# Near attention of a metaformer: the exponential, the spreading and the write at other steps of the pipeline

## The chip, the cores and the metric

The kernel runs on one core of a Trainium2 chip. The metric is the device time of one execution in microseconds (us). A core has five engines with an instruction queue each: PE (matmul), DVE (VectorE), ACT (ScalarE), POOL (GpSimd) and SP (SyncE), which in this kernel issues transfers. Sixteen DMA engines carry the transfers.

## The reference

Four layers of a metaformer work on an image batch `x` of shape (4, 64, 64, 128). The change touches the first half of layer 0 alone, a deformable attention in which each pixel attends to nine sampled pixels, in four groups of 32 channels with dilations 1, 3, 5 and 7. Cut to what matters:

```python
qkv = conv2d_depthwise(x @ w_qkv + b_qkv)
mask = sigmoid(conv1x1(pconv(q_img, pconv_mask_w), w_mask, b_mask))
for i in range(4):
    off = conv1x1(pconv(q_img, pconv_off_w[i]), w_off[i], b_off[i])
    dil = 2 * i + 1
    k_list.append(deform_sample(kv[0, :, i], off, mask, dil, dil * PAD))
    v_list.append(deform_sample(kv[1, :, i], off, mask, dil, dil * PAD))
...
attn = softmax(einsum('bgnc,bgckn->bgnk', qf, ks_), axis=-1)
out = einsum('bgnk,bgckn->bgnc', attn, vs_)
return out @ w_proj + b_proj
```

`deform_sample` samples bilinearly at a tap's place plus its learned offset and multiplies by the mask. The other layers (an expert-choice FFN, a triangle update and a recurrent layer, a Fourier attention and a pair attention, each with a mixture of experts) are the same in both kernels.

## The kernel before

When no offset is larger than 1, the kernel takes `deformable_near`. There every tap reads a 3 x 3 neighbourhood of its undisplaced place, so a query's keys and values lie in a fixed window, and bilinear sampling is a weighting with "hat" functions of the offset.

The work is cut into 128 steps; one step is two image rows, 128 query pixels, which lie on the 128 partitions. Four steps make a chunk `c`; there are 32 chunks, eight for each of four images. One loop over `T` runs all stages of the pipeline at once. What a pass does for step `T` or for a chunk is told by `step(T, first, do, every)`: it calls `do(n)` for `n = (T - first) / every` where that is a whole number in range. In order of a chunk's life:

- Four passes of `product` (L773, PE): products of queries and keys in PSUM `S`; `copy_products` (L783, ACT) moves them to `band`, of which there are two sets. `products` (L744, ACT) prepares the next queries.
- `hats_of_rows` and `hats_of_columns` (ACT, L700, L704), `masked` and `hat_products` (POOL, L722, L731) make the interpolation weights `H`, two buffers.
- At step 4c+4, `attention` (L785 to L812, DVE): shift the bands by predicated copies (L792), weight with `H` and reduce to logits `lg` (L794, L801), subtract the largest (L809 to L811).
- At step 4c+7, `spread` (L814 to L836): the exponential on ACT (L817), then on DVE the sum, the reciprocal and the scaling (L818 to L820), then `A`, the weight of each pixel of the window: nine products (L824) for dilations 3, 5 and 7, three into `shared` (L830) and a reduce (L834) for dilation 1. `A` has two buffers.
- At step 4c+9, `write` (L841, SP): four transfers of `A` to a ring of three buffers `dd` in DRAM.
- At `LAG - 2` = 12 steps after its own number, `read_dense` (L850, SP): four transfers bring a step's rows back from `dd` as a dense matrix `D`, four buffers in turn. This turns a layout by query into one by key.
- At `LAG` = 14 steps after its own number, `values`, `transpose` (L884 on PE, L886 on ACT) and `weigh` (L904, PE) multiply `D` with the values `vb` (L862, SP, seven buffers); after every fourth step, `values_done` (L916), `projection` (L925 to L929) and `store` (L936, SP) finish a chunk. The residual `xg` is loaded by SP (L876) into two buffers in turn; its buffer is free once the store of the chunk before last has landed.

SP also loads queries (`q`, L759), offsets (`of`, L696) and keys (`kpad`, L752). All of SP's transfers stand in one queue, in the order in which they are built.

Within one pass the order of the engines' instructions is set by two means: the order of the calls, and `tc.issue_after`, which keeps what is built inside it from going ahead of a named instruction. `behind()` names the last block of PE; `after[0]` is the last copy of products of this pass. Otherwise a scheduler orders instructions by what they wait for, so an instruction need not stand where its call does.

Of the kernel before, what the change touches and what calls it, by code (L numbers as in the profile page):

```python
# [12 lines left out]
AF = mybir.ActivationFunctionType  # L13
# [347 lines left out]
def window(ap, off, dims):  # L361

    return bass.AP(ap.tensor, ap.offset + off, [list(ap.ap[0])] + dims)


def stage_deformable(k, x, y, w_qkv, b_qkv, w_dw, b_dw, pconv, w_offT, b_off, grid, masks, w_proj, b_proj):

    nc, tc = k.nc, k.tc
    with ExitStack() as octx:  # L380
        dr = octx.enter_context(tc.tile_pool(name="da_d", bufs=1, space=DRAM))
        fp = octx.enter_context(tc.tile_pool(name="da_f", bufs=1))
        qd = [dr.tile([128, 4096], F32, tag=f"qd{b}", name=f"qd{b}") for b in range(4)]
        kd = [dr.tile([128, 4096], F32, tag=f"kd{b}", name=f"kd{b}") for b in range(4)]
        vd = [dr.tile([80, 84, 128], F32, tag=f"vd{b}", name=f"vd{b}") for b in range(4)]
        od = [dr.tile([128, 32, 81], F32, tag=f"od{b}", name=f"od{b}") for b in range(4)]
        far = deformable_project(k, fp, x, qd, kd, vd, od, w_qkv, b_qkv, w_dw, b_dw, pconv, w_offT, b_off)
        with tc.If(far > 0) as branch:
            deformable_general(k, x, y, w_qkv, b_qkv, w_dw, b_dw, pconv, w_offT, b_off, grid, w_proj, b_proj)
        with branch.Else():  # L390
            deformable_near(k, dr, x, y, qd, kd, vd, od, masks, w_proj, b_proj)
# [217 lines left out]
def deformable_near(k, dr, x, y, qd, kd, vd, od, masks, w_proj, b_proj):  # L609
# [19 lines left out]
    nc, tc = k.nc, k.tc  # L629
# [5 lines left out]
    with ExitStack() as ctx:  # L635
# [44 lines left out]
        Hs, bands, outs, vblocks, logits, ofs, hat_of, queries = {}, {}, {}, {}, {}, {}, {}, {}  # L680
# [3 lines left out]
        def behind():  # L684

            return tc.issue_after(last[0].ins) if last[0] is not None else ExitStack()

        def block(do, *args):

            with behind():  # L690
                last[0] = do(*args)
# [32 lines left out]
        def hat_products(c, groups):  # L724

            if 0 in groups:
                Hs[c] = sm.tile([128, 4, 36, 12], F32, tag="H", name="H")
            H = Hs[c]
            hy, hx, _ = hat_of[c]
            for g in groups:  # L730
                nc.gpsimd.tensor_tensor(  # L731
                    H[:, g].rearrange("p n (a c) -> p n a c", a=4), window(hy, 144 * g, [[4, 36], [1, 4], [0, 3]]),
                    window(hx, 108 * g, [[3, 36], [0, 4], [1, 3]]), op=ALU.mult,
                )

        def products(T):
            i = T % 32
            c, t = divmod(T, 4)
            if t == 0:
                bands[c] = [sm.tile([128, 3, 4, 4, CW[g]], F32, tag=f"band{g}", name=f"band{g}") for g in range(4)]  # L740
            qm = qms[T % 2]
            q = queries[T // 4]
            for h in range(2):
                nc.scalar.copy(  # L744
                    window(qm, 256 * h, [[32, 2], [72, 4], [1, 8]]),
                    q[:, 2 * (i % 4) : 2 * (i % 4) + 2, 32 * h : 32 * h + 32].rearrange("p y (m x) -> p y m x", m=4),
                )

        def rows_of_keys(n):

            b, h = divmod(n, 4)
            nc.sync.dma_start(  # L752
                kpad[:, 8 + 16 * h : 24 + 16 * h, 8:72], kd[b].rearrange("p (y x) -> p y x", x=64)[:, 16 * h : 16 * h + 16, :]
            )

        def rows_of_queries(n):
            b, h = divmod(n, 8)
            queries[n] = sm.tile([128, 8, 64], F32, tag="q", name="q")
            nc.sync.dma_start(queries[n], qd[b].rearrange("p (y x) -> p y x", x=64)[:, 8 * h : 8 * h + 8, :])  # L759
# [25 lines left out]
        def attention(c):  # L785
# [25 lines left out]
            nc.vector.tensor_tensor(lg, lg, each, op=ALU.subtract)  # L811
            logits[c] = lg, m, me, taps, wide, each  # L812

        def spread(c):  # L814
            H = Hs.pop(c)
            lg, m, me, taps, wide, each = logits.pop(c)
            nc.scalar.activation(lg, lg, AF.Exp, scale=32 ** (-0.5))  # L817
            nc.vector.tensor_reduce(m, taps, axis=AX.XY, op=ALU.add)  # L818
            nc.vector.reciprocal(me, wide)
            nc.vector.tensor_tensor(lg, lg, each, op=ALU.mult)  # L820
            A = As[c % 2]
            for g in range(1, 4):
                for ty in range(3):
                    nc.vector.tensor_tensor(  # L824
                        window(A[g], ty, [[12 * DIL[g], 12], [3, 4], [12, 3]]), window(H, 432 * g + 144 * ty, [[12, 12], [3, 4], [1, 3]]),
                        window(lg, 36 * g + 12 * ty, [[1, 12], [0, 4], [0, 3]]), op=ALU.mult,
                    )

            for tx in range(3):
                nc.vector.tensor_tensor(  # L830
                    window(shared, 13 * tx, [[60, 12], [3, 4], [12, 3]]), window(H, 12 * tx, [[36, 12], [3, 4], [1, 3]]),
                    window(lg, tx, [[3, 12], [0, 4], [0, 3]]), op=ALU.mult,
                )
            nc.vector.tensor_reduce(  # L834
                window(A[0], 0, [[1, 3], [60, 4], [3, 20]]), window(shared, 0, [[240, 3], [60, 4], [3, 20], [1, 3]]), axis=AX.X, op=ALU.add
            )  # L836
# [96 lines left out]
        def store(some):  # L933
            for o in some:
                _, b, c, xg = o
                nc.sync.dma_start(tokens(y, b, 4 * c, 4), xg)  # L936
                stores.remove(o)

        def step(T, first, do, every=1):
            n = T - first  # L940
            if 0 <= n < 128 and n % every == 0:
                do(n // every)

        LAG = 14
        for h in range(4):
            rows_of_keys(h)
        rows_of_queries(0)
# [2 lines left out]
        products(0)  # L950
        for T in range(128 + LAG):
            now[0] = T
            with behind():
                step(T, -1, products)
                step(T, -5, offsets, 4)
                step(T, 2, masked, 4)
                step(T, 2, lambda c: hat_products(c, (0, 1)), 4)
                step(T, 3, lambda c: hat_products(c, (2, 3)), 4)
                step(T, 4, attention, 4)
                step(T, 7, spread, 4)  # L960
                step(T, 9, write, 4)
                step(T, LAG - 2, read_dense)
                step(T, LAG, values)
            V, P = 0 <= T - LAG, T < 128
            late = [o for o in stores if o[0] <= T - 2]
            if V:
                block(transpose, T - LAG)
            if P:
                block(product, T)
            if project:  # L970
                block(projection, *project.pop())
            if V:
                block(weigh, T - LAG)
            with behind():
                store(late)
                step(T, 0, copy_products)
                with tc.issue_after(after[0].ins):
                    step(T, 0, hats_of_rows, 4)
                    step(T, 1, hats_of_columns, 4)
                step(T, LAG, values_done)  # L980
                if T % 4 == 1 and T < 124:
                    rows_of_queries(T // 4 + 1)
                if T < 96:
                    b, i = divmod(T, 32)
                    for h in range(4):
                        if i == min(8 * h + 13, 31):
                            rows_of_keys(4 * (b + 1) + h)
# [1639 lines left out]
```

## Time and profile before

| what | us |
|---|---|
| three runs: lowest, median, highest | 7522.86, 7536.76, 7555.75 |
| profiled execution: its time | 7520.84 |
| profiled execution: its span | 7519.0 |
| near stage in the span | about 680 to 1668 |
| of it: first writes of A to the ring (L841) | 731.20, 753.21, 775.93, 796.84 |
| of it: 26 chunks, from the write at 829.27 to that at 1583.50 | 754.23 |
| busy in those 754.23: PE, DVE, ACT, POOL | 627.95, 594.68, 423.87, 191.34 |
| busy share of the whole span: PE, DVE, ACT, POOL | 86%, 64%, 38%, 20% |

Three views are used below. The page is one profiled execution in numbers: busy time, 40 slices of the span, the costliest groups. A view of waits says for one engine what its idle time ended on, added up. A timeline lists runs of equal instructions in order of start: start, duration, engine, line, operation, output, inputs, and in square brackets the idle time before it with what ended it. For SP the duration is the time in which its queue hands the transfers out. `L841` is line 841 of the kernel before. The near stage is an eighth of the time, so shares over the whole span say little about it; windows inside it do.

### The profile page before, as it was taken

Reading aid. Unit: us, or ns where it says so; the run is one execution under the profiler, and the core shown is the slowest. Engines: PE = TensorE matmul, PEld = TensorE weight load, DVE = VectorE, ACT = ScalarE, POOL = GpSimd, SP = SyncE. Lnnn points to the kernel's source line nnn. Section 1 sums busy time; section 2 is a strip of 40 time slices with the busy share of each in tenths; the row PEclk is TensorE's granted clock in tenths of the full one; section 3 lists DMA queues with packets and bytes.
Section 4 is the critical chain, followed back from the end, with each engine's and each line's share of the span. In section 5 each row is a group of like instructions: output and inputs, shape, how many; then the busy total and the mean of one; then the engine's idle time right before and its main releaser. Section 6 shows DMA issues by size and latency. Waiting matters only on the chain. (4 is left out here: it accounts for less than half of the span.)

```text
span 7519.0 us, 156903 instructions
## 1 busy us (share of the span) xinstructions
PE 6475.0 (86%) x63791; PEld 3490.8 (46%) x63791; DVE 4812.9 (64%) x10774; ACT 2842.8 (38%) x6717; POOL 1518.8 (20%) x1218
## 2 busy tenths in 40 slices
PE   7996888866688789799989988798897997998989
PEld 3443666654455553255555555445224234252244
DVE  2113877754577437588756566674885876857877
ACT  3332555543243326411156665564013022040055
POOL 0001222210011100055522221253012111120135
PEclk9997888987889899899989899797997997988989
DMA  4436788871300130300000000001111111111101
GB/s 120 98 89 195 210 246 242 244 227 60 137 1 2 34 67 9 116 23 23 25 10 9 9 10 4 9 1 42 34 25 50 26 39 34 27 32 41 23 23 31
DMA packets 673783, 498.10 MB, mean 66 GB/s; under 512 B 296822, under 2 KB 588600, under 8 KB 669208
## 3 DMA queue, kind: packets, MB, share of 16 engines
q1 hardware_dynamic: 510158, 399.80, 18.9%
q10 hardware_dynamic: 162890, 88.11, 4.4%
q8 instruction: 509, 8.34, 0.5%
q14 instruction: 226, 1.85, 0.1%
HBM read 335.28 MB, written 152.33 MB: 65 GB/s over the span
## 5 line engine op out<-in xcount | busy, mean ns | idle before, releaser
L2496 DVE TENSOR_TENSOR t<-S,q 128x1536 f32<-128x1536 f32 (+3 forms) x608 | 1157.0, 1949 | 120.7 <-PE S L2484 115.5
L2484 PE MATMUL S<-R,L 32*128 32x512 f32 x4096 | 734.6, 651 | 90.1 <-DMA R<-wd 78.6
L2512 PE MATMUL acc<-t,sum 128*32 128x512 f32 x4096 | 639.6, 608 | 0.0
L2198 PE MATMUL pe<-ew,yT 128*128 128x512 f32 x1024 | 480.6, 604 | 25.2 <-DVE xs L2204 22.3
L1797 PE MATMUL acc<-w,attT 128*64 128x264 f32 x4096 | 485.2, 390 | 11.0 <-DVE w L1793 11.0
L2484 PEld LDWEIGHTS S<-R,L 32*128 32x128 f32 x4096 | 200.4, 186 | 611.2 <-issue 280.1
L2518 ACT COPY agg<-acc 128x512 f32<-128x512 f32 x32 | 18.8, 586 | 1192.6 <-DMA L<-pd 855.4
L792 DVE COPY_PREDICATED band<-bit,band 128x384 f32<-128x384 int32 (+11 forms) x384 | 312.5, 929 | 186.4 <-ACT band L783 149.8
L773 PE MATMUL S<-kpad,qm 32*64 32x192 f32 (+3 forms) x8192 | 365.8, 405 | 72.4 <-ACT band L783 37.7
L2204 DVE SCALAR_TENSOR_TENSOR xs<-pe,gate,xs 128x128 f32<-128x128 f32 x1024 | 333.1, 346 | 96.9 <-PE pe L2198 80.3
L1790 POOL TENSOR_TENSOR w<-xtl,ei 128x528 f32<-128x528 f32 x256 | 332.1, 1319 | 310.5 <-ACT ei L1789 202.5
L1793 DVE TENSOR_TENSOR w<-xtl,pe 128x1056 f32<-128x1056 f32 x256 | 320.4, 1251 | 99.5 <-ACT ei L1789 88.6
L1797 PEld LDWEIGHTS acc<-w,attT 128*64 128x64 f32 x4096 | 283.5, 137 | 197.1 <-DVE w L1794 38.3
L2207 ACT ACTIVATE sc<-pe,gate 128x128 f32<-128x128 f32 x1024 | 291.2, 375 | 199.5 <-PE pe L2198 192.4
L773 PEld LDWEIGHTS S<-kpad,qm 32*64 32x64 f32 x8192 | 265.6, 151 | 128.8 <-issue 65.3
L514 PE MATMUL dw<-pad,diag 32*32 32x512 f32 x6912 | 307.4, 612 | 13.2 <-issue 7.3
L884 PE MATMUL pt<-ident,D 128*128 128x128 f32 x1536 | 259.8, 319 | 66.3 <-DMA D<-dd 48.4
L2512 PEld LDWEIGHTS acc<-t,sum 128*32 128x32 f32 x4096 | 92.7, 108 | 458.4 <-issue 436.1
L2198 PEld LDWEIGHTS pe<-ew,yT 128*128 128x128 f32 x1024 | 185.6, 193 | 232.1 <-issue 151.5
L2527 POOL TENSOR_TENSOR o<-o,bf 128x512 f32<-128x512 f32 x32 | 40.7, 1271 | 1228.5 <-ACT o L2526 1228.5
L886 ACT COPY dt<-pt 128x512 f32<-128x512 f32 x384 | 205.5, 595 | 146.2 <-PE pt L884 145.7
L884 PEld LDWEIGHTS pt<-ident,D 128*128 128x128 f32 x1536 | 214.6, 203 | 87.6 <-DMA D<-dd 52.3
(520 smaller groups left out, 12716.7 us busy)
## 6 DMA issues: line engine op xcount, KB each, us to landing
vb<-vd SPq DMA_DIRECT2D x272, 256.0 KB
D<-dd SPq DMA_DIRECT2D x128, 192.0 KB
D<-dd SPq DMA_DIRECT2D x128, 168.0 KB
D<-dd SPq DMA_DIRECT2D x128, 144.0 KB
w<-in_e_weight_dram ACTq DMA_DIRECT2D x16, 1024.0 KB
w<-in_e_weight_dram SPq DMA_DIRECT2D x16, 1024.0 KB
wd<-s SPq DMA_DIRECT2D x32, 512.0 KB
D<-dd SPq DMA_DIRECT2D x128, 120.0 KB
```

What stands on the lines that cost most here:

```text
L514: nc.tensor.matmul(acc[g][32 * c : 32 * c + 32], diag[r, j, tap, :], pads[j][r, y0 : y0 + 8, tx : tx + 64], start=(tap == 0), stop=(tap == 8),
L773: ins = nc.tensor.matmul(acc[g][64 * h : 64 * h + 64].rearrange("p (a s) c -> p a s c", a=3), qm[rows, h, m, :], keys, start=(m == 0), sto ...
L792: nc.vector.copy_predicated(flat[:, :, 0:n], bit[:, 0, :, i : i + 1].to_broadcast([128, 48, n]), flat[:, :, s : s + n])
L884: ins = nc.tensor.transpose(pt[:, g, :], D[:, g, ty : ty + 382 : 3], k.ident)
L1790: nc.gpsimd.tensor_tensor(w2[:, 2:4], xt[:, 2:4, 0:2], window(ei, 0, [[0, 2], [0, 2], [1, 132]]), op=ALU.mult)
L1793: nc.vector.tensor_tensor(w1, xt[:, :, 1:3], window(pe, 0, [[0, 4], [0, 2], [1, 132]]), op=ALU.mult)
L1797: nc.tensor.matmul(acc[b // 2][64 * (b % 2) : 64 * (b % 2) + 64], attT[:, b // 2, hp, 64 * (b % 2) : 64 * (b % 2) + 64], src[:, b].rearran ...
L2198: nc.tensor.matmul(pe[h].rearrange("p e c -> p (e c)"), yT[:, 128 * t : 128 * t + 128], ew[:, 4 * h : 4 * h + 4, :].rearrange("p e c -> p ...
L2204: nc.vector.scalar_tensor_tensor(xt, pe[0][:, e, :], gate[:, t, e : e + 1], xt, op0=ALU.mult, op1=ALU.add)
L2484: nc.tensor.matmul(S[:, j, :], Ls[n % 2][r, ag, :], Rs[n % 2][r, ag].rearrange("p x y -> p (x y)"), start=True, stop=True)
L2496: nc.vector.tensor_tensor(t[:, j0:j1].rearrange("p u (x y) -> p u x y", x=8), S[:, j0:j1].rearrange("p u (x y) -> p u x y", x=8), qf[:, q0 ...
L2512: nc.tensor.matmul(acc[0][32 * h : 32 * h + 32, :], sum4, t[:, j, :], start=(u < 4), stop=(u >= 60))
```

## The change

`spread` is split. The exponential becomes a function of its own, `exponential`, and is issued at step 4c+7 inside the `issue_after(after[0])` at the end of the pass, that is, not ahead of that pass's last copy of products. The rest of `spread` is issued one step later (4c+8), `write` one step later (4c+10). `LAG` is 15, so that the values of a step are used one step later, and the loop has 143 passes in place of 142. `read_dense` stays at twelve steps after its own number, now `LAG - 3`: a step's dense rows are read three steps ahead of their use. The number of buffers, the instructions and the transfers are the same. Of the built order on DVE it can be said that the logits of chunk c+1 now stand between those of chunk c and the spreading of chunk c.

```diff
--- before.py
+++ after.py
@@ -811,10 +811,13 @@
             nc.vector.tensor_tensor(lg, lg, each, op=ALU.subtract)
             logits[c] = lg, m, me, taps, wide, each
 
+        def exponential(c):
+            lg = logits[c][0]
+            nc.scalar.activation(lg, lg, AF.Exp, scale=32 ** (-0.5))
+
         def spread(c):
             H = Hs.pop(c)
             lg, m, me, taps, wide, each = logits.pop(c)
-            nc.scalar.activation(lg, lg, AF.Exp, scale=32 ** (-0.5))
             nc.vector.tensor_reduce(m, taps, axis=AX.XY, op=ALU.add)
             nc.vector.reciprocal(me, wide)
             nc.vector.tensor_tensor(lg, lg, each, op=ALU.mult)
@@ -941,7 +944,7 @@
             if 0 <= n < 128 and n % every == 0:
                 do(n // every)
 
-        LAG = 14
+        LAG = 15
         for h in range(4):
             rows_of_keys(h)
         rows_of_queries(0)
@@ -957,9 +960,9 @@
                 step(T, 2, lambda c: hat_products(c, (0, 1)), 4)
                 step(T, 3, lambda c: hat_products(c, (2, 3)), 4)
                 step(T, 4, attention, 4)
-                step(T, 7, spread, 4)
-                step(T, 9, write, 4)
-                step(T, LAG - 2, read_dense)
+                step(T, 8, spread, 4)
+                step(T, 10, write, 4)
+                step(T, LAG - 3, read_dense)
                 step(T, LAG, values)
             V, P = 0 <= T - LAG, T < 128
             late = [o for o in stores if o[0] <= T - 2]
@@ -977,6 +980,7 @@
                 with tc.issue_after(after[0].ins):
                     step(T, 0, hats_of_rows, 4)
                     step(T, 1, hats_of_columns, 4)
+                    step(T, 7, exponential, 4)
                 step(T, LAG, values_done)
                 if T % 4 == 1 and T < 124:
                     rows_of_queries(T // 4 + 1)
```

## The prediction

> **What bounds the kernel now.** The change touches one stage, the near attention of layer 0, so I read the page's 40 slices first. This is their DMA row:
>
> ```profile
> DMA  4436788871300130300000000001111111111101
> ```
>
> A slice is 188 us. Slices 4 to 8 (about 680 to 1668 us of the span) are the near stage, and nowhere else is DMA so busy. The view of windows gives an undisturbed piece of it (columns: us, busy PE, PE weight load, DVE, ACT, POOL, TensorE clock, DMA share, GB/s):
>
> ```profile
> 1100.00:1350.00 250.00, 203.89 (x5847) 167.06 (x5847) 193.65 (x381) 140.89 (x421) 59.67 (x58) 0.89 0.81 242
> ```
>
> PE at 82%, DVE at 77% and DMA at 81%: three near-ties, no compute engine full. So I read who waits, between 830 and 1580 us, in the views of waits of ACT, PE and SP (waited for: us, times, longest):
>
> ```profile
> ACT lg L817 <- DVE lg L811: 84.4, 23, 6.3
> ```
>
> ```profile
> PE out L904 <- issue: 40.2, 31, 3.3
> PE pt L884 <- DMA D<-dd: 38.6, 54, 3.1
> ...
> PE S L773 <- ACT band L783: 5.2, 6, 2.1
> ```
>
> ```profile
> SPq L876 <- DMA x<-xg: 49.1, 23, 2.8
> ```
>
> The first line is what catches the eye: ACT stands 84.4 us for the logits before the exponential, with the copies of PE's products behind it. But PE, which would have to suffer from that, waits for ACT only 15.5 us in that stretch (5.2 here; 6.9, 2.6 and 0.8 in lines of that view not shown). It waits longer for dense rows. One such place, in the timelines of ACT, PE and DVE:
>
> ```profile
> 1196.01 0.32 ACT L817 ACTIVATE lg<-lg 128x144 f32<-128x144 f32 x1 [4.94 <-DVE lg L811]
> ```
>
> ```profile
> 1195.36 0.35 PE L884 MATMUL pt<-ident,D 128*128 128x128 f32 x1 [3.05 <-DMA D<-dd]
> ```
>
> ```profile
> 1200.63 3.11 DVE L830 TENSOR_TENSOR shared<-H,lg 128x144 f32<-128x144 f32 x3
> 1203.77 0.90 DVE L834 TENSOR_REDUCE A<-shared 128x240 f32<-128x720 f32 x1
> ```
>
> ACT's 4.94 us end at 1196.0, but PE stood for D until 1195.4. Two stalls lie side by side, and removing ACT's moves nothing there. Why D is late shows in SP's queue, one chunk of it:
>
> ```profile
> 1180.12 4.16 SPq L841 DMA_DIRECT2D dd<-A  x4
> 1184.38 2.00 SPq L862 DMA_DIRECT2D vb<-vd  x2
> 1186.47 0.54 SPq L696 DMA_DIRECT2D of<-od  x1
> 1187.06 1.26 SPq L862 DMA_DIRECT2D vb<-vd  x2
> 1188.52 3.46 SPq L850 DMA_DIRECT2D D<-dd  x4
> 1192.06 0.41 SPq L759 DMA_DIRECT2D q<-qd  x1
> 1192.58 1.41 SPq L936 DMA_DIRECT2D x<-xg  x1
> 1194.08 2.60 SPq L850 DMA_DIRECT2D D<-dd  x4
> 1199.33 0.39 SPq L876 DMA_DIRECT2D xg<-in_x_dram  x1
> 1199.82 3.10 SPq L862 DMA_DIRECT2D vb<-vd  x4
> 1203.01 5.30 SPq L850 DMA_DIRECT2D D<-dd  x8
> 1208.41 4.95 SPq L841 DMA_DIRECT2D dd<-A  x4
> ```
>
> From write to write is 28.29 us. The rows hold dd 4.16, vb 2.00 + 1.26 + 3.10, D 3.46 + 2.60 + 5.30, small loads 0.54 + 0.41 + 1.41 + 0.39: 24.63 in all. 2.65 is a hole (1196.68 to 1199.33: the xg load waits for an x store), 1.0 small gaps. DVE had A ready at 1204.67 (1203.77 + 0.90), and SP came for it at 1208.41, 3.7 us later. In this stretch I find SP 1 to 16 us behind DVE at every write. The transposes of D(57) ended at 1178.2, and the next rows for that buffer were issued at 1194.1, 16 us after it came free. So SP's queue, an in-order list of transfers that keeps the DMA engines at 0.81, sets the end of a chunk; DVE, ACT and, mostly, PE are pulled along. From the write at 829.27 to the one at 1583.50 are 26 chunks: 29.0 us each.
>
> **What the Trainium skill says.** "DMA: Bandwidth & Descriptors", section "Anatomy of one DMA — SWDGE (gpsimd) path": a semaphore wait happens on the issuing sequencer before dispatch, the DMA engines only consume their queues. It is stated for another path; the hole of 2.65 us before the xg load, with vb and D behind it, shows the same on SP. "SBUF — State Buffer", section "Who interferes with whom": a VectorE operation with two SBUF inputs contends with GpSimd reads, a tensor_reduce never. The trace agrees: three shared products took 3.11 us above, beside POOL, and 0.94 at 1610.59 us, alone; the reduce took 0.90 both times.
>
> **The change, part by part.** No instruction is added or removed: 32 exponentials, 128 writes and 512 dense reads in either kernel. All of it is order.
>
> 1. The exponential of chunk c goes from step 4c+7 ahead of the copies, where the built order puts it before the copy of step 4c+5, to behind the copies of step 4c+7. ACT's wait of 84.4 us goes. What is late next: PE's rows of D, at the same time. Of the 15.5 us that PE waits for ACT I count 5.2 + 0.8 as owed to the exponential and give a third of it, 2 us, to the end; the rest is bought by D.
>
> 2. Spread moves behind the following attention. DVE's work per chunk was 15.16 (attention, 1180.81 to 1195.97) + 0.40 (exponential) + 8.30 (spread, to 1204.67) = 23.9 us. The 0.40 goes. In the built order the tail of attention c+1 and the head of spread c are interleaved, and POOL's products of H for chunk c+2 must wait for the buffer that spread c reads, so the overlap on shared (3.11 against 0.94) and on the nine A products (3.26 against 2.45) mostly goes: up to 3.0 us of DVE. DVE isn't the bound: 0. If that cover is gone (SP faster), it would be worth up to 3.4.
>
> 3. Write one step later, in chunk time: A is ready about 21 us after attention c+1 starts, 24 if the contention stays. Read by steps, from A's end to the write is about as much as before, 0 to 3 us more. The write stands in SP's queue with the 16 reads of the next chunk and the vb loads behind it; if it has to wait, they all do. Seen slack 1 to 16 us, so 0, bounded by 0 and 2 us a chunk.
>
> 4. LAG 15 with reads at T - 12: the same step in the loop, so the reads are not moved in it, but each is used one step later, and the write, one step later too, still comes five steps ahead of the first use. The four D buffers come free one step later relative to the read. SP is 16 us behind that already, so 0. One drain step more: the drain at the end (1610 to 1650 us) is itself paced by D reads, 5.3 us per two steps, and one write now stands right before the reads that need it: about +3 us once.
>
> 5. SP's order, from the built kernels: before, write, 2 vb, of, 2 vb, D4, q, x, D4, xg, 4 vb, D8; after, write, 2 vb, q, of, D4, 2 vb, D4, 2 vb, x, D4, xg, 2 vb, D4. The same 16 D, 8 vb, 4 writes, the same bytes; vb is spread out, and the xg load still follows one D4 after the store. The hole of 2.65 stays, 0; bounded by -1 (more time between store and load) and +2.2 (below).
>
> 6. Start: up to 797 us SP does wait for A: its writes begin at 731.20, 753.21, 775.93 and 796.84, so DVE sets the pace at about 22 us. After, the first A is finished some 16 us later, but the copies of chunk 1 no longer stand behind the first exponential (5.37 us) and the second (4.79), and values start a step later. By my count of steps the first transpose comes at about 762 instead of 766.8: -5 us, once, bounded by -7 and +10.
>
> Sum: -2 - 5 + 3 = -4 us. Against the profiled execution's 7520.84 (span 7519.0 + 1.84): 7517. The median of the runs shown is 7536.76, 15.9 above that execution; against it the same -4 gives 7533.
>
> **The rivals.** *Faster: the ACT stall is the bound after all.* For it: 84.4 us over 23 chunks is 3.7 each, PE is the busiest engine, and its 40.2 us of "issue" ahead of L904 have no visible cause. If a chunk is set by PE, it can fall from 29.0 towards its busy time, 24.2 (627.95 over the 26 chunks, by the view of windows), plus 2.5 of issue gaps (65.3 over 26): 26.7. Against it: the DMA share, and SP behind DVE at each write. I take 2 us a chunk over 28 chunks: -56, 7481.
>
> *Slower: SP's new order makes the x round trip dearer.* A pair of vb and, in about 12 chunks, a kpad load now stand ahead of the store. If SP's in-order wait for the store (2.65 us) grows by the time that two more vb need (2 x 256 KB at 242 GB/s is 2.2 us), and kpad, whose following four vb took 5.74 us at 1109.5 against 3.10 here, falls on it, a chunk costs 2.2 more: 28 x 2.2 = +62, 7599. It decides from 1.35 us a chunk (38 over 28). Against it: what is ahead of the store isn't between the store and the load.
>
> *Slower: the write waits for DVE.* Slack of 3.7 us here, at times 1. If the spread moved behind an attention takes SP from 3.7 ahead to 1.3 short in each chunk, 27 x 1.3 = +35: about 7570.
>
> **How the numbers follow.** 0.5% of 7536.76 is 38 us, about what a measurement of this kernel can tell from no change: same is 7499 to 7574. The forecast, 7533, has 0.63; the faster rival 0.20; the two slower ones 0.12 and 0.05. The forecast's own range, from the bounds of parts 3, 5 and 6, is 7505 to 7565, mostly same. The second slower rival straddles the border and gives 0.01 to same; so faster 0.20, same 0.64, slower 0.16. The range over all, 7487 to 7587, leaves out half of the faster rival and most of the first slower one.
>
> **What would show it.** Right: the chunk from dd write to dd write stays at 28.5 to 29.5 us; ACT's wait at L817 falls below 10 us; PE's waits for D and its issue gaps stay or grow by as much as its waits for ACT shrink; shared takes about 1 us; SP still arrives after A is done. The first rival: a chunk of 27 us or less with PE above 85%. The second: the wait of L876 above 100 us in the stage. The third: SP's dd write waiting for DVE L834 in most chunks. The forecast is wrong if the near stage, 988 us, changes by more than 38.

## The result, and the profile after

The changed kernel takes 7559.47 us (median of 7 runs, 7545.16 to 7572.25); the kernel before, in its runs beside it, 7536.76 (7 runs). The ratio is 1.0032, with a 95% interval of 1.0016 to 1.0048: slower by about 23 us, where 4 us less was forecast. The profiled execution of the changed kernel took 7557.5 us (span 7555.5) against 7520.84.

Where the time went can be read from the first transposes of single steps (line 884 before, 887 after). The first of step 0 starts at 759.9 us (before 766.8), that of step 8 at 814.3 (823.0), of step 116 at 1619.8 (1599.5), of step 127 at 1687.7 (1658.8). So the start is 8.7 us earlier, the 27 chunks in between lose 29 us, about 1.1 each, and the drain loses another 8.6. Up to the first transpose of step 127 this is +28.9 of the 36.7 by which the two profiled executions differ; the rest comes after it. From here on "a chunk" is the mean from step 24 to step 112, 22 chunks: 29.15 us before, 30.09 after. These are means of one profiled execution each. Two of the experiments below, `xg3` and `late_vshape`, left SP's order as it is before and after, and had 29.22 and 30.11, so differences below about 0.1 us say nothing.

The same window as before, in the changed kernel (columns as there):

```profile
1100.00:1350.00 250.00, 198.01 (x5566) 159.56 (x5566) 176.42 (x361) 134.04 (x399) 63.40 (x57) 0.86 0.83 233
```

PE and DVE are less busy than before (203.89 and 193.65), and the DMA share has risen from 0.81 to 0.83, while the rate fell from 242 to 233 GB/s. DMA is busier for fewer bytes. The granted TensorE clock between steps 24 and 112 was lower, 0.876 in place of 0.895. That is not what cost the time: `xg3` had 0.876 too, with the chunk of before.

The views of waits, 830 to 1580 us, of PE, ACT and SP:

```profile
PE pt L887 <- DMA D<-dd: 80.1, 101, 3.1
PE out L907 <- issue: 35.6, 21, 3.9
PE out L907 <- DMA vb<-vd: 14.5, 3, 5.9
```

```profile
ACT qm L744 <- PE S L773: 168.8, 96, 3.5
ACT dt L889 <- PE pt L887: 161.5, 114, 5.9
```

```profile
SPq L939 <- POOL H L731: 40.2, 12, 6.1
SPq L879 <- DMA x<-xg: 35.1, 17, 3.1
```

ACT's wait for the logits, 84.4 us before, is not in its list any more; ACT now waits for PE alone. PE's waits for ACT's copies of 15.5 us are gone too, but its wait for dense rows has doubled, from 38.6 to 80.1.

SP's first line is new: the store of x (L939) is held in SP's queue, for POOL by this view. POOL is unlikely to be what it waits for: the store handed out for 5.63 us from 1229.30 on had its result from POOL at 1213.75. The ten long ones among these stores all stand right behind a load of keys (`kpad`, L752), and what stands there was handed out slowly before as well (2.5 to 3.8 us, now 4.6 to 6.3). Nor is it where the time was lost: from write to write, the ten chunks with a load of keys (of chunks 4 to 28) took 31.1 us before and 31.4 after, the fifteen without one 27.8 and 29.3. With other transfers of SP's queue as marks, the chunks without one still lose 1.0 to 1.4 us.

DVE does what was expected of it (timeline):

```profile
1200.71 0.92 DVE L833 TENSOR_TENSOR shared<-H,lg 128x144 f32<-128x144 f32 x3
1201.67 0.90 DVE L837 TENSOR_REDUCE A<-shared 128x240 f32<-128x720 f32 x1
```

The shared products take 0.92 us in place of 3.11, and A is ready at 1202.6. SP's queue for the chunk around it, which has no load of keys:

```profile
1182.85 3.33 SPq L844 DMA_DIRECT2D dd<-A  x4
1186.53 1.71 SPq L865 DMA_DIRECT2D vb<-vd  x2
1188.34 1.10 SPq L759 DMA_DIRECT2D q<-qd  x1
1189.53 0.38 SPq L696 DMA_DIRECT2D of<-od  x1
1190.01 2.64 SPq L853 DMA_DIRECT2D D<-dd  x4
1192.74 1.25 SPq L865 DMA_DIRECT2D vb<-vd  x2
1194.08 2.73 SPq L853 DMA_DIRECT2D D<-dd  x4
1197.44 1.73 SPq L865 DMA_DIRECT2D vb<-vd  x2
1199.42 0.38 SPq L939 DMA_DIRECT2D x<-xg  x1
1200.40 3.04 SPq L853 DMA_DIRECT2D D<-dd  x4
1206.56 0.39 SPq L879 DMA_DIRECT2D xg<-in_x_dram  x1
1207.05 1.94 SPq L865 DMA_DIRECT2D vb<-vd  x2
1209.04 2.65 SPq L853 DMA_DIRECT2D D<-dd  x4
1211.79 3.35 SPq L844 DMA_DIRECT2D dd<-A  x4
```

SP comes for A at 1211.8, 9 us after it is ready: the write doesn't wait for DVE. What is new is the neighbourhood: twice in this chunk (1192.7 and 1197.4) value blocks are handed out directly behind a dense read. In the chunk shown of before that happened nowhere: behind the reads stood q, the hole before xg, other reads, or the write.

The trace has a record of each packet too. Packets of 1536 bytes occur only in the fourth read of a step; packets of 2048 bytes are value blocks and q. Their mean times, between steps 8 and 116:

```
                      1536 bytes   2048 bytes   DMA engines' time per MB (mean of 16)
before                  73.2 ns     103.1 ns     3.32 us
after                   83.4 ns     108.3 ns     3.49 us

1536 bytes by what stands behind the read in SP's queue, ns (number of reads)
before   write 70 (30)   read 69 (24)   q 77 (19)   xg after its hole 71 (24)   values 93 (9)
after    write 73 (27)   values 91 (57)   xg after its hole 71 (14)   xg at once 83 (9)
```

In the second part a read is given the packets that start between 1.6 us after its hand-out and 1.6 us after that of the next fourth read. Before, values stand right behind a read too, but only in three short stretches (981 to 1021, 1218 to 1259 and 1453 to 1492 us), and there the packets are as slow as after.

That gave theory J (in the first expectations, A: the order in SP's queue): a value-block load directly behind a dense read slows both, and as DMA is what a chunk waits for, the chunk with them. The rival, B, was that the late exponential, spreading and write cost it on ACT, DVE or POOL.

### The profile page after: what moved, and what is told of

Same layout as the page of the kernel before. It is cut to its first block, busy times and chain, and to the rows that moved or that the text cites. A ratio compares the mean times of both kernels' runs of the same rounds, so it can differ in the third digit from the quotient of the medians.

```text
span 7555.5 us, 156872 instructions
## 1 busy us (share of the span) xinstructions
PE 6484.5 (86%) x63791; PEld 3494.5 (46%) x63791; DVE 4791.3 (63%) x10774; ACT 2847.7 (38%) x6717; POOL 1547.4 (20%) x1218
## 5 line engine op out<-in xcount | busy, mean ns | idle before, releaser
L792 DVE COPY_PREDICATED band<-bit,band 128x384 f32<-128x384 int32 (+11 forms) x384 | 379.8, 1100 | 248.6 <-ACT band L783 214.1
L773 PE MATMUL S<-kpad,qm 32*64 32x192 f32 (+3 forms) x8192 | 346.7, 399 | 59.5 <-ACT band L783 25.6
L887 PE MATMUL pt<-ident,D 128*128 128x128 f32 x1536 | 282.5, 330 | 109.3 <-DMA D<-dd 104.8
```

The lines of the kernel that those rows point to most:

```text
L773: ins = nc.tensor.matmul(acc[g][64 * h : 64 * h + 64].rearrange("p (a s) c -> p a s c", a=3), qm[rows, h, m, :], keys, start=(m == 0), sto ...
L792: nc.vector.copy_predicated(flat[:, :, 0:n], bit[:, 0, :, i : i + 1].to_broadcast([128, 48, n]), flat[:, :, s : s + n])
L887: ins = nc.tensor.transpose(pt[:, g, :], D[:, g, ty : ty + 382 : 3], k.ident)
```

## The experiments

Names with "early" change the kernel before, names with "late" the changed one; `exp_alone` and `xg3` change the kernel before. Sixteen runs were made; ratios are to the kernel before on the same chip, with 95% intervals.

**Halves of the change.** `late_two` puts one number back:

```diff
-                step(T, LAG - 3, read_dense)
+                step(T, LAG - 2, read_dense)
```

> The changed kernel with one number put back: dense rows are read at LAG - 2 = 13, two steps ahead of use, so that SP's queue has the value blocks in groups of four again and not in pairs between the reads; exponential, spreading and write stay late. Theory A (the order of reads and value blocks in SP's queue makes the transfers themselves longer, 1536-byte reads 83.6 ns against 73.4 in the kernel before): a chunk falls from 30.1 back to about 29.0 us and, with the start 7 us earlier, the ratio to the kernel before is 0.996 to 1.000; 1536-byte packets at about 74 ns. Theory B (the late exponential, spreading and write on ACT, DVE and POOL cost it): the ratio stays at 1.003, a chunk at 30 us.

Measured 1.0049 (1.0030 to 1.0067), a chunk of 30.65, 1536-byte packets at 84.4 ns. Neither expectation: the value blocks stand in fours now, but one four still stands behind a read (about 96 ns in the 36 reads of 27 chunks with values right behind them), and the write splits another group of reads. It has fewer such reads than the changed kernel (1.4 a chunk against 2.1) and a longer chunk, so their number alone doesn't give the loss.

`early_three` is the other half:

```diff
-        LAG = 14
+        LAG = 15
-                step(T, LAG - 2, read_dense)
+                step(T, LAG - 3, read_dense)
```

> The other half: the kernel before with LAG 15 and reads at LAG - 3 = 12, exponential, spreading and write as before. SP's queue has the pairs of value blocks between the reads, as in the changed kernel. Theory A: a chunk of about 30.1 us, and the start gains nothing (values begin a step later), so the ratio is 1.004 to 1.007; 1536-byte packets at about 83 ns. Theory B: a chunk of 29.0 us, ratio 1.000 to 1.001 for the extra step.

Measured 1.0078 (1.0061 to 1.0095), a chunk of 30.72, 1536-byte packets at 85.4 ns. B is out as the whole cause: nothing of the exponential, spreading or write was moved here, and the kernel is slower than the changed one (part of that is a start 15 us later: step 8 at 838.1 us). It has three reads per chunk with values behind them.

`exp_alone` moves only the exponential, split off from `spread` as in the changed kernel:

```diff
+                    step(T, 6, exponential, 4)
```

> The kernel before with only the exponential moved: it is issued at the end of step 4c+6 behind that step's copies, spreading stays at 4c+7, write at 4c+9, LAG 14. ACT's wait of 84 us for the logits should be gone. Theory A (SP and its transfers set a chunk): ratio 0.997 to 1.001. Rival (ACT's stall was the bound): chunk of 27 us, ratio 0.992 to 0.994. Theory B predicts a part of the loss here: 1.001 to 1.003.

Measured 1.0039 (1.0026 to 1.0052), a chunk of 30.31. ACT's wait fell to 1.5 us between 830 and 1580, and the kernel got slower. SP's order, which a scheduler makes, had moved along with it: 1.5 reads per chunk have values directly behind them (about 95 ns), another 0.5 only the xg load between (88 ns). So the number expected under A was missed, and the run doesn't separate the exponential from SP's order; it does show that without ACT's stall a chunk isn't 27 us.

**The hole before xg.** `xg3` gives xg three buffers (`bufs=3`).

> The kernel before with three buffers for the residual xg in place of two: the xg load no longer waits for an x store, a hole of 2.05 us per chunk in SP's queue (53.2 us over 26 chunks). If SP's queue as an issuing engine sets a chunk, the hole is worth 1.5 to 2 us of 29.0: ratio 0.993 to 0.995. If the 16 DMA engines, busy for 0.81, are the bound and go on during the hole, it is worth under 0.5 us: ratio 0.998 to 1.000.

Measured 1.0006 (0.9997 to 1.0015). It decides nothing: with three buffers three loads are issued at the start, each later one moves up by a chunk, and it waits for a store at the same place (53.9 us, before 49.1).

**One neighbourhood put in.** `early_xg` moves one transfer of the kernel before:

```diff
-                nc.sync.dma_start(inputs[0], tokens(x, b, i - 1, 4))
+                with tc.issue_after(queued[0].ins):
+                    nc.sync.dma_start(inputs[0], tokens(x, b, i - 1, 4))
```

`queued[0]` is the last dense read built.

> The kernel before with one transfer moved: the xg load is held behind the dense reads that stood after it. SP's queue becomes write, 2 values, of, 2 values, read, q, x, read, 4 values, 2 reads, xg: the hole in which the xg load waited for the x store (2.05 us per chunk) goes, and in its place a value-block load stands directly behind a dense read once per chunk, except where kpad is between. All else as before. Theory J (that neighbourhood slows both transfers on full engines): the gain of the hole is given back, 1536-byte packets of that read rise from 71 to 90 ns or more, chunk 29.2 to 29.8 us, ratio 1.000 to 1.004. Rival (a hole in SP's queue is time lost, the neighbourhood costs nothing): 1.5 to 2 us less per chunk, ratio 0.992 to 0.995.

Its timeline of SP shows the hole gone and the neighbourhood in its place:

```profile
1198.23 3.20 SPq L850 DMA_DIRECT2D D<-dd  x4
1201.52 2.96 SPq L862 DMA_DIRECT2D vb<-vd  x4
1204.85 6.97 SPq L850 DMA_DIRECT2D D<-dd  x8
1211.87 0.45 SPq L877 DMA_DIRECT2D xg<-in_x_dram  x1
```

Measured 1.0025 (1.0017 to 1.0034), a chunk of 29.79; the read before the values takes about 98 ns a packet, at a place where it was 71. This is the cleanest run for J: ACT, DVE and POOL run the same instructions in the same order as before, one transfer of 33 was moved, a hole of 2 us was removed, and the chunk is 0.64 us longer; over some 29 chunks that is 19 us, which the medians show (7555.64 against 7534.32). How the slower packets lengthen the chunk here is open, though. PE's waits for dense rows, 830 to 1580 us, are what they were before (38.6):

```profile
PE pt L885 <- DMA D<-dd: 39.2, 58, 1.8
```

**All such neighbourhoods taken out.** In `late_grouped` the eight value-block loads of a chunk stand behind the write, and the reads behind them:

```diff
-                step(T, LAG - 3, read_dense)
                 step(T, LAG, values)
+                with tc.issue_after(queued[0].ins) if queued[0] is not None else ExitStack():
+                    step(T, LAG - 3, read_dense)
...
+            if i == 0 or i % 4 == 3:
...
+                    with tc.issue_after(queued[0].ins) if queued[0] is not None else ExitStack():
+                        value_block(n)
```

> The changed kernel with SP's order fixed by hand: the eight value-block loads of a chunk stand in one group right behind the write of A, and the dense reads behind them, so that no dense read is directly followed by a value-block load (write, 8 values, read, of, read, q, read, x, read, xg). Exponential, spreading, write and LAG 15 as changed. Theory J (a value-block load right behind a dense read slows both): 1536-byte packets at 68 to 76 ns, a chunk of 28.5 to 29.1 us, ratio 0.997 to 1.000. Rival (late spreading and write themselves, or reads three steps ahead): a chunk of 30 us, ratio 1.003 to 1.005.

Measured 1.0037 (1.0024 to 1.0050). The packets are as fast as before (73.3 and 101.4 ns) and the chunk is 29.52, but step 8 starts at 840.3 in place of 814.3: the first value blocks came late too. `late_grouped2` mends that alone.

> late_grouped with the first value blocks loaded at the start of the stage again, as in the changed kernel (in late_grouped they came late and cost the start about 26 us). Theory J: packets as in late_grouped (1536 bytes at 73 ns), a chunk of 29.2 to 29.5 us, and the start of the changed kernel, so 15 to 25 us less than late_grouped: ratio 0.999 to 1.002, below the changed kernel's 1.003. Rival: late_grouped's chunk of 29.5 comes from its late start, and the ratio is 1.003 to 1.005.

```profile
1182.78 2.77 SPq L844 DMA_DIRECT2D dd<-A  x4
1185.61 6.17 SPq L865 DMA_DIRECT2D vb<-vd  x8
1191.87 2.63 SPq L853 DMA_DIRECT2D D<-dd  x4
1194.68 0.33 SPq L696 DMA_DIRECT2D of<-od  x1
1195.34 2.95 SPq L853 DMA_DIRECT2D D<-dd  x4
```

Measured 1.0015 (1.0007 to 1.0023), a chunk of 29.54, packets at 73.6 and 101.1 ns. The packets are as fast as before, and more than half of the loss per chunk (0.94 to 0.39 us) is gone. What makes up the other 0.4 us is not settled: PE still waits longer than before for dense rows (58.7 us between 830 and 1580, before 38.6) and for values (18.1, before 6.0), and theory B, the late spreading and write, is not excluded for this part.

**Is it the transfers at all?** `early_halfD` and `late_halfD` halve the length of every dense read, in the two orders. They leave out half of the window. (Theory E, that eight of the sixteen DMA engines are full, is taken up in the next part.)

```diff
-                    dense[t][:, g, 12 * (7 - d) : 12 * (7 - d) + P],
+                    dense[t][:, g, 12 * (7 - d) : 12 * (7 - d) + P // 2],
```

(the source's `[1, P]` likewise).

> The kernel before with dense reads of half the length: each row brings its first P/2 elements, the rest of D stays zero. Same 33 transfers per chunk, same packets, same waits; left out is half of the attention weights' window, so the output is another. Theory E (the eight DMA engines that carry the dense reads are full and set a chunk): their load falls from 31.4 us per chunk by about 6 to 25.4, DMA is no longer the bound, PE is, with 24.2 busy and 2.5 of issue: a chunk of 25.5 to 27.2 us, ratio 0.988 to 0.993. Rival (the number of transfers that SP has to issue, or PE with ACT and DVE, sets a chunk): 29 us, ratio 0.999 to 1.001.

> The changed kernel with the same halved dense reads (the same part is left out). Theory E with J (the change loses only through its order of transfers): with DMA off the bound it loses nothing any more, the start is 5 to 8 us earlier and ACT doesn't wait for the logits: equal to early_halfD or up to 30 us faster, ratio 0.984 to 0.993. Rival (late spreading costs on DVE, ACT or POOL): 0.2 to 0.4% above early_halfD.

Measured 0.9902 (0.9886 to 0.9919) and 0.9867 (0.9844 to 0.9889); chunks of 26.76 and 26.32; medians 7455.00 and 7428.52. PE's waits in `early_halfD`, 830 to 1560 us:

```profile
PE S L773 <- ACT band L783: 30.5, 17, 4.0
```

PE waits for dense rows 2.8 us only, and now it does wait for ACT's copies; in `late_halfD` that line is absent. So in the kernel before the dense reads do set the chunk, with the number of SP's transfers as it was. Not all of the 2.4 us is waiting, though: PE was busy for 23.2 us a chunk in place of 24.2, at a granted clock of 0.930 in place of 0.895, and why is open.

`late_halfD` is 26 us below `early_halfD` by medians of four runs each (18 in the profiled pair; the spread of the runs leaves some 20 either way). With whole reads the same two orders differ by +23. This is not the change's worth without any transfers: in `late_halfD` PE still waits 24.8 us for dense rows and 16.9 for values. But with shorter reads the order of the changed kernel no longer loses, which speaks against theory B as the main cause.

**Which part of DMA is full?** The packet records say how many packets are in flight. Between 850 and 1590 us, before, dense reads had more than 10 at once for 0.005 of the time in which they had any, and 8 far more often than any other number; packets of 2048 bytes had more than 10 for 0.35 of it. Of all packets together, between steps 24 and 112, fewer than 6 were in flight for 0.006 of the time, and 10 or fewer for 0.39. The Trainium skill, "DMA: Bandwidth & Descriptors", section "Why a DMA increments its semaphore by 16 and not by 1", says how many engines a transfer uses: the largest number up to 16 that divides the slowest dimension of both sides (the outermost one that isn't 1). A dense read's source has 8 there, a value block's 32. So a mean share of 0.81 can be eight engines that are full and eight that are half idle (theory E).

`late_vshape` was to put the value blocks on eight engines too.

```diff
-[[10752, 32], [128, 4], [1, 512]]
+[[43008, 8], [10752, 4], [128, 4], [1, 512]]
```

> The changed kernel with the same value-block bytes read in the same order, but the source pattern written with 8 as its slowest dimension in place of 32. Theory E (a transfer spreads over as many of the 16 DMA engines as divide the slowest dimension, so the dense reads, with 8, use eight engines only, and these eight are full): the value blocks, 512 packets of 2048 bytes per block pair and so 1024 a chunk, then load the same eight engines twice as much, 1024 x 105 ns / 16 = 6.7 us more per chunk: a chunk of 35 to 37 us, ratio 1.020 to 1.030, and never more than about ten 2048-byte packets of them in flight. Rival (the pattern's notation doesn't matter, the DMA share of 0.82 is what 16 engines give): no difference from the changed kernel, 1.002 to 1.005.

Measured 1.0027 (1.0016 to 1.0038), with more than ten 2048-byte packets in flight for 0.19 of their time (changed kernel 0.18). The two outer dimensions are one run of 32 at one pitch, so the split is unlikely to have reached the transfer; not a test of E, only a repeat of the changed kernel.

`early_uni` and `late_uni` lay the ring out so that a read has one pitch:

```diff
-                    bass.AP(m.tensor, m.offset, [[4 * P + 12, 128], [P, 4], [1, 12 * W[g]]]),
+                for t in range(4):
+                        bass.AP(m.tensor, m.offset + t * P, [[64 * P, 8], [4 * P + 12, 16], [1, 12 * W[g]]]),
...
-                    bass.AP(m.tensor, m.offset + t * P, [[16 * (4 * P + 12), 8], [4 * P, 16], [1, P]]),
+                    bass.AP(m.tensor, m.offset + t * P, [[4 * P, 128], [1, P]]),
```

> The kernel before with another layout of the ring dd: groups of 16 pixels lie 64 P elements apart in place of 64 P + 192, so that a dense read is 128 rows at one pitch (slowest dimension 128), and the write, now in four transfers per group, has 8 as slowest dimension. Same bytes, 12 more transfers per chunk. Theory E: dense reads on 16 engines (7.7 us a chunk as a mean over 16, in place of 15.4 on eight), writes on eight (8.2 in place of 4.1), so the load of the fullest engines falls from 31.1 to 27.5 and a chunk from 28.8 to 25.5 to 27 us, where PE's 24.2 busy plus 2.5 is next: ratio 0.988 to 0.994. Rival (SP's issuing of transfers is the bound): 12 more transfers at 0.4 us, a chunk of 32 to 34 us, ratio 1.012 to 1.02.

> The changed kernel with the same other layout of the ring. Theory E: as early_uni, and where the eight engines are no longer full the order of SP's queue costs less and ACT's removed wait and the start come through: 0.984 to 0.992 of the kernel before. Rival (the loss of the change is in ACT, DVE or POOL): it stays 0.3% above early_uni.

Measured 1.0068 (1.0054 to 1.0083) and 1.0088 (1.0072 to 1.0103), chunks of 31.24 and 31.10. The packets in flight moved as the rule says: dense reads now had more than 10 for 0.53 of their time, writes more than 11 for 0.006 of theirs (before 0.16). But the gain didn't come. The share fell to 0.77 and 0.76, and fewer than 6 packets were in flight for 0.08 and 0.10 of the time (before 0.006): DMA has more idle time than before. SP hands out its 45 transfers for 26.3 us per chunk, against 22.4 before; that this is the new bound fits, but isn't shown.

`early_pair` and `late_pair` keep that layout and read two steps in one transfer, 37 per chunk, into two buffers of two steps each:

```diff
-                    bass.AP(m.tensor, m.offset + t * P, [[4 * P, 128], [1, P]]),
+                    bass.AP(m.tensor, m.offset + t * P, [[4 * P, 128], [P, 2], [1, P]]),
```

> early_uni with the dense reads of two steps in one transfer (the rows at one pitch allow it): 37 transfers per chunk in place of 45, and 33 in the kernel before. Theory E plus a bound of SP's queue at about 0.58 us a transfer: the fullest engines have 28 us of load in place of 31.4, SP some 22 plus 5 of waits: a chunk of 27 to 28.3 us, ratio 0.991 to 0.997. Rival (a pair has to wait for both of its buffers, so that it comes late for PE): 29.5 us or more, ratio above 1.001.

> late_uni with the dense reads of two steps in one transfer, two steps ahead (a pair can't be read three ahead with two pairs of buffers). Theory E: as early_pair, and with the start 5 to 8 us earlier 0.990 to 0.996. Rival: as for early_pair, above 1.001.

Measured 0.9974 (0.9963 to 0.9985) and 0.9989 (0.9980 to 0.9997), chunks of 28.76 and 28.85. `early_pair`, at 7513.62 us against 7534.32 beside it, is faster than both kernels of this case. Its chunk is 0.4 us shorter, not the 1 to 2 expected, at 247 GB/s between 1100 and 1350 us (before 242), and its step 8 starts 8.9 us earlier. So the eight engines alone do not set the chunk; what relieving them is worth by itself is not separated from the fewer and longer reads.

`early_pool` and `late_pool` issue the reads of two groups from POOL:

```diff
-                nc.sync.dma_start(
+                (nc.sync, nc.gpsimd)[g % 2].dma_start(
```

> The kernel before with the dense reads of the second and fourth group issued from POOL in place of SP. Theory E: if POOL's transfers go to other engines than the same eight, the load of those eight falls from 31.4 to about 27.3 us and a chunk to 26 to 27.5: ratio 0.990 to 0.995. If they go to the same eight, or POOL's queue is held up by the reads' waits for PE with the interpolation products behind them: ratio 1.000 to 1.02.

> The changed kernel with the same two groups' dense reads issued from POOL. Theory E with J: as early_pool, and with reads three steps ahead POOL's waits for PE come earlier: equal to early_pool or up to 20 us faster. Rival: 0.3% above early_pool, as the changed kernel is above the one before.

Measured 1.0024 (1.0013 to 1.0034) and 1.0060 (1.0043 to 1.0077). POOL's waits in `early_pool`, 830 to 1580 us:

```profile
POOL D L850 <- PE pt L884: 412.5, 75, 13.7
```

Between steps 24 and 112, 15 to 17 packets are in flight for 0.45 of the time (before 0.31). POOL's reads travel mostly in packets of 4608 bytes, so their times don't compare with before; SP's own do, and they are slower: 1344 bytes take 74.0 ns in place of 63.3, 2048 bytes 109.7 in place of 103.1. The chunk is 30.10.

Put together, with the reads that have values directly behind them counted from SP's order between steps 24 and 112:

```
                 such reads a chunk   chunk us   1536 bytes   ratio
before                 0.4             29.15       73.2       1
early_xg               0.9             29.79       80.8       1.0025
late_grouped2          0               29.54       73.6       1.0015
changed                2.1             30.09       83.4       1.0032
exp_alone              1.5             30.31       83.8       1.0039
late_two               1.4             30.65       84.4       1.0049
early_three            3.0             30.72       85.4       1.0078
```

The time of a packet and that of a chunk go together, but for `late_grouped2`. The count of such reads is a coarser guide: `exp_alone` and `late_two` have fewer than the changed kernel and lose more.

## Why the prediction was wrong

The reading of the profile held: transfers set the chunk (`early_halfD`, with the reservation made there), ACT's wait was covered by PE's wait for dense rows, DVE wasn't on the path. Step by step:

- Part 1, ACT's wait, -2 us. Its wait went (4.4 us left in the stage), and with it PE's waits for ACT. While transfers set the chunk this is bought by D, as written; `late_halfD` against `early_halfD` shows that with shorter reads the change as a whole, this part included, gains some 26 us.
- Part 2, DVE: shared took 0.92 us as expected, and it moved nothing, as expected.
- Part 3, the write: from chunk 4 on SP comes about 6 us or more after A is ready. Right.
- Part 4, the drain, +3: it was +8.6. Why was not tried.
- Part 5 is the step that failed: "The same 16 D, 8 vb, 4 writes, the same bytes; vb is spread out ... The hole of 2.65 stays, 0". The order was read right, values behind reads included, and the hole stayed in most chunks (3.1 us in the one shown), but equal bytes were taken for equal time. In place of the 0, packets of 1536 bytes went from 73.2 to 83.4 ns, and the chunk by 0.94 us, some 28 us over the stage. `early_xg` shows the same with one transfer moved and nothing else, `late_grouped2` that another order brings back more than half; the rest stays open. The bound of +2.2 held the size, but it was reasoned from another mechanism, so that the measured 7559.47 lies inside the forecast's own range of 7505 to 7565 is luck.
- Part 6, the start, -5: -6.9 at the first transpose, -8.7 at step 8. Right, and a little small.

The sum in the terms of the prediction is -9 for the start, +29 for the chunks and +9 for the drain in the profiled executions, against -5, 0 and +3 (and -2 for part 1); part 5 alone is more than the medians' 23 us.

Of the rivals, the first (ACT's stall as the bound) is refuted by the changed kernel itself and by `exp_alone`: the stall is gone, the chunk longer. The second had the right place, SP's new order, and a wrong mechanism: the wait of the xg load didn't grow, it fell from 49.1 to 35.1 us. The load of keys did fall on the x store, as it said, but the loss lies in the chunks without one. The third didn't occur. Two of the forecast's own tests failed: the chunk, to stay at 28.5 to 29.5 us, was 30.1, and PE's waits for dense rows grew by 41.5 us, where at most the 15.5 of its waits for ACT were to go there.

## What to carry to other kernels

When transfers set the pace, a reordering of one queue is not free because the bytes are the same: list what stands behind what before and after, and price the neighbourhoods from packet times; the trace of before already held nine reads with values behind them, at 93 ns. A mean DMA share of 0.81 need not mean room: here a chunk was 2.4 us shorter with half of the dense reads' bytes. To see whether a change of order loses on the compute engines or on transfers, run both orders with the bound eased: here the same change was some 26 us better with short reads and 23 us worse with whole ones.

## What the runs showed of the hardware

- The same dense read took about 70 ns a 1536-byte packet with a write (a transfer out of SBUF) behind it, and 90 to 98 with a load of value blocks behind it. Why these two hinder each other was not tried.
- Reads with 8 as slowest dimension had more than 10 packets in flight for 0.005 of their time, the same bytes with 128 for 0.53 of it.
- More packets of the dense reads in flight did not raise the rate much: 242 GB/s before, 247 in `early_pair`. With half of the reads issued from POOL, SP's 1344-byte packets took 74.0 ns in place of 63.3.
- The same three DVE products took 3.11 us beside POOL's products of H and 0.92 us just ahead of them.
